# Four residual layers over a 256 x 256 image: the spectra of the kernels' rows stored without a copy, in quarters of the channels, and a third buffer for the sums

## The chip, the core and the metric

The kernel runs on one core of one Trainium2 chip. The metric is the device time of one execution, in microseconds (us). The core has a matrix engine (TensorE, PE in the profile), a vector engine (VectorE, DVE), an activation engine (ScalarE, ACT), a general engine (GpSimd, POOL), a queue engine that issues transfers (SyncE, SP), and 16 DMA engines that move data between HBM and the on-chip memory, SBUF. Each compute engine works through its instructions in the order in which they were built and waits on semaphores. Results of TensorE land in PSUM.

## The reference, cut to what matters

The image x is 1 x 256 x 256 x 128, float32. Four layers follow one another, each of the form x = x + layer(group norm of x).

```python
def _gn(v, G=32, eps=1e-5):
    B_, H_, W_, C_ = v.shape
    g = v.reshape(B_, H_, W_, G, C_ // G)
    m = jnp.mean(g, axis=(1, 2, 4), keepdims=True)
    s = jnp.var(g, axis=(1, 2, 4), keepdims=True)
    return ((g - m) / jnp.sqrt(s + eps)).reshape(v.shape)

x = x + _L0_conv_ref(_gn(x), ...)   # attention along rows, 4 heads of 32, with a pair bias
x = x + _L1_conv_ref(_gn(x), ...)   # 16 steps of a gated recurrence
x = x + _L2_conv_ref(_gn(x), ...)   # triangle product
x = x + _L3_conv_ref(_gn(x), ...)   # 3 x 3 convolution and a dense layer
```

The change touches what layers 0 and 1 need. Layer 0 needs mean and variance of x per group of four channels before anything else. Layer 1 multiplies by the two-dimensional Fourier transforms of two small complex kernels, A and B, of 7 x 7 taps for each of 64 channels, padded to 256 x 256:

```python
def _pad_and_fft(kr, ki, h, w, k):
    kern = kr + 1j * ki
    ph = (h - k) // 2
    pw = (w - k) // 2
    padded = jnp.pad(kern, ((0, 0), (ph, h - k - ph), (pw, w - k - pw)))
    return jnp.fft.fft2(padded, axes=(-2, -1))
A_f = _pad_and_fft(A_real, A_imag, h, w, k)
B_f = _pad_and_fft(B_real, B_imag, h, w, k)
```

## The kernel before

The image is held channel-major in HBM between the stages: 128 channels on the partitions, 65536 pixels along them. The stages run one after another:

- A first pass over x (`statistics`), for sums and sums of squares.
- A second pass (`attention`, its loop over m) that transposes x, normalises it, and stores xT, znT and the pair bias.
- The attention itself (`attend_bounded`), the recurrence, the triangle product and the convolution.

**The first pass.** x comes in 32 chunks of 2048 pixels, 1 MB each, issued by SP (line 243). Most go through a ring of three buffers (`xin`); the last ones in the order of work stay in buffers of their own (`kept`, six of them, line 349), since the second pass begins with them and needn't load them again. Each chunk has two halves of 128 x 1024. For each half VectorE subtracts a shift (written at line 246; the profile shows it as L224, the wrapper that pins it), ScalarE squares the result (line 249; L54 in the profile, the helper), and TensorE adds both up in one PSUM tile, `acc`, with matmuls by ones of 32 columns. The sums of a half take in its differences, `xs`, and the squares, `sq`, of the half before. `xs` and `sq` come from the pool `p0`, which has two buffers of each. These steps are pinned: each engine takes them in the order of the text. In the end VectorE copies `acc` (line 263), and the group statistics follow.

**The spectra of the rows.** The same loop makes the one-dimensional transform of the kernels' seven rows, for A and then for B (`kernel_rows`). After chunks 4, 5, 7, 8, 10, 11, 13 and 14 it calls `spectrum` for A, after 16, 17, 19, 20, 22, 23, 25 and 26 for B. One call treats two channels of each quarter of the 64: TensorE makes `ph` (eight small matmuls, behind the sums of that chunk), and ScalarE copies it to a tile H (line 191), with the 14 rows of quarter k on partitions 32k to 32k+13. H is 128 x 256 x 16, one buffer: 256 points of the transform, 16 channels of a quarter. When a spectrum is complete, GpSimd puts the four quarters of 16 channels beside one another: eight copies (line 197) of 14 x 128 x 16 into the tile HH, four to each half of the 256 points. Two stores (line 198), one to a half, take HH to HBM, to `HD_`, laid out as [2 kernels, 14 rows, 256 points, 64 channels].

**Where the spectra are read.** The recurrence treats four image rows in a block, 64 blocks. `load` fetches for each block, on SP's queue, the image twice (`xf` and the two halves of `xc`) and the spectra for those four rows into `hs`, 128 x 2 x 64 (line 882): four loads, for each kernel n and each r, with two rows of 64 channels for each of 14 partitions. `za` (kernel A) and `zb` (kernel B) are matmuls that use `hs` as weights. The order of the work in a block is a written list of steps with their lags; the loads of a block are issued one block ahead, and `hs` has two buffers, which come free after `zb`.

**Weights.** `attention_weights` is a generator that the loop of the first pass advances: after chunk 1 its loads are out, and at `n == 28` its small computations are recorded. They are not pinned.

Of the kernel before, what the change touches and what calls it, by code (L numbers as in the profile page):

```python
# [9 lines left out]
F32 = mybir.dt.float32  # L10
# [7 lines left out]
P = 128  # L18
N = 256
NPIX = N * N  # L20
NCH = NPIX // 512
NH, HD = 4, 32
KS = 7
HC = P // 2
# [6 lines left out]
class Kernel:  # L31
# [132 lines left out]

    def kernel_rows(self, sp, ps, HD_):


        nc, I = self.nc, self.i
        CG = HC // 4
        tu = self.load(sp, I["c_rows"], "tu")  # L170
        HH = sp.tile([P, N // 2, HC], F32, name="HH")
        H, ka = [], []
        for n, (re, im) in enumerate((("A_real", "A_imag"), ("B_real", "B_imag"))):
            kr, ki = (I["L1_conv_" + y].rearrange("c p q -> p c q") for y in (re, im))
            k = sp.tile([3 * KS, HC, 32], F32, name=f"ka{n}")
            nc.gpsimd.memset(k, 0.0)
            for p0, q0, src in ((0, 0, kr), (0, KS, ki), (KS, 0, ki), (2 * KS, KS, kr)):
                nc.gpsimd.dma_start(k[p0:p0 + KS, :, q0:q0 + KS], src)
            ka.append(k)

        pin = lambda f: lambda *a, **k: self.tc.keep_in_program_order(f(*a, **k))

        def spectrum(g):
            n, g0 = divmod(2 * g, CG)
            if not g0:
                H.append(sp.tile([P, N, CG], F32, name="H"))
            ph = ps.tile([P, 2, N], F32, name="ph", bufs=2)
            for j in range(2):
                for k in range(4):
                    pin(self.mm)(ph[32 * k:32 * k + 32, j], ka[n][:, CG * k + g0 + j, :], tu)  # L190
            pin(nc.scalar.copy)(H[n][:, :, g0:g0 + 2].rearrange("q u c -> q c u"), ph)
            if g0 + 2 == CG:
                for h in range(2):
                    o = slice(64 * n + 32 * h, 64 * n + 32 * h + 2 * KS)
                    u = slice(h * N // 2, (h + 1) * N // 2)
                    for k in range(4):
                        nc.gpsimd.tensor_copy(HH[o, :, CG * k:CG * (k + 1)], H[n][32 * k:32 * k + 2 * KS, u])
                    nc.gpsimd.dma_start(HD_[n][:, u], HH[o])
        return spectrum

    def statistics(self, wp, weights, HD_, kept, src):

        nc, I = self.nc, self.i
        V = nc.vector
        x = I["x"].rearrange("b h w c -> (b h w) c")
        NM, KEPT = NPIX // 2048, len(kept)
        mv = wp.tile([P, 2], F32, name="mvx")
        with ExitStack() as c:  # L210
            sp = c.enter_context(self.pool(name="sp", bufs=1))
            io = c.enter_context(self.pool(name="p0", bufs=2))
            ps = c.enter_context(self.pool(name="p0s", bufs=1, space=PSUM))
            row = sp.tile([1, P], F32, name="row")
            nc.sync.dma_start(row, x[0:1])
            shc = self.column(sp, x[0:1].rearrange("o c -> (o c)"), "shc")
            ones = sp.tile([P, P], F32, name="ones0")
            V.memset(ones, 1.0)
            psh = ps.tile([P, 4, P], F32, name="psh", tag="ph", bufs=2)
            self.mm(psh[:, 0], ones[0:1], row)  # L220
            sh = sp.tile([P, P], F32, name="sh")
            V.tensor_copy(sh, psh[:, 0])
            acc = ps.tile([P, 512], F32, name="acc")
            pin = lambda f: lambda *a, **k: self.tc.keep_in_program_order(f(*a, **k))  # L224
            last, count = None, [0, 0]

            def add_up(*pair):
                for h in range(2):
                    for j, t in enumerate(pair):
                        if t is not None:  # L230
                            o = 64 * j + 32 * h
                            pin(self.mm)(acc[o:o + 32], ones[:, :32], t[:, h * 512:(h + 1) * 512],
                                    start=count[j] < 2, stop=count[j] >= 4 * NM - 2)
                            count[j] += 1

            order = list(range(KEPT, NM)) + list(range(KEPT))
            spectrum, made = None, 0
            for n, m in enumerate(order):
                if m < KEPT:
                    xin = kept[m]  # L240
                else:
                    xin = io.tile([P, 2, 1024], F32, name="xin", bufs=3)
                nc.sync.dma_start(xin, src(m))
                for b in range(2):
                    xs = io.tile([P, 1024], F32, name="xs")
                    pin(V.tensor_tensor)(xs.rearrange("p (t c) -> p t c", t=8), xin[:, b].rearrange("p (t c) -> p t c", t=8),
                                    sh.unsqueeze(1).to_broadcast([P, 8, P]), ALU.subtract)
                    sq = io.tile([P, 1024], F32, name="sqx")
                    pin(self.act)(sq, xs, AF.Square)

                    add_up(xs, last)
                    last = sq
                if n == 1:
                    spectrum = self.kernel_rows(sp, ps, HD_)
                    next(weights)
                elif n == 28:
                    weights = next(weights)
                elif n >= 4 and n % 3 and made < 16:
                    spectrum(made)
                    made += 1  # L260
            add_up(None, last)
            accs = sp.tile([P, 512], F32, name="accs")
            V.tensor_copy(accs, acc)
            sel = sp.tile([P, 2], F32, name="sel")
            V.memset(sel, 0.0)
            V.memset(sel[:64, 0:1], 1.0 / 32 / NPIX)
            V.memset(sel[64:, 1:2], 1.0 / 32 / NPIX)
            pm = ps.tile([P, 2], F32, name="pmx")
            for t in range(4):
                self.mm(pm, accs[:, t * P:(t + 1) * P], sel, start=t == 0, stop=t == 3)  # L270
            V.tensor_copy(mv, pm)
            e = sp.tile([P, 1], F32, name="ex")
            V.tensor_tensor(e, mv[:, 0:1], mv[:, 0:1], ALU.mult)
            V.tensor_tensor(mv[:, 1:2], mv[:, 1:2], e, ALU.subtract)
            V.tensor_tensor(mv[:, 0:1], mv[:, 0:1], shc, ALU.add)
        return mv, weights
# [58 lines left out]

    def attention(self, wp, later, xT, x1T, znT, biasD, HD_, stats1, shift1):
        nc, tc, I = self.nc, self.tc, self.i
# [4 lines left out]
        with ExitStack() as c:  # L342
# [3 lines left out]
            c1 = c.enter_context(ExitStack())  # L346
            kp = c1.enter_context(self.pool(name="kp", bufs=1))

            kept = [kp.tile([P, 2, 1024], F32, name=f"kept{m}") for m in range(6)]
            mv, (w, (lns, lnb), wo, small) = self.statistics(wp, self.attention_weights(wp), HD_, kept, src)  # L350
            with self.pool(name="awq", bufs=2, space=PSUM) as ps0:
                ab, mg, _ = self.group_affine(wp, ps0, None, self.g4, "0", True, mv=mv)
# [14 lines left out]
            io = c1.enter_context(self.pool(name="a1", bufs=3))  # L367
# [70 lines left out]
                    nc.sync.dma_start(biasD[:, s:s + 512], bi[32 * k:32 * k + NH])  # L438

            tc.keep_in_program_order(self.table(LN_EXP))  # L440
            for m in range(6, 8):
                load(m)
            turn(0)
            centre(0, 0)
# [372 lines left out]
    def recurrence(self, x1T, x2T, HD_, stats1, shift1, stats2, shift2):  # L817
# [3 lines left out]
        nc, tc, I = self.nc, self.tc, self.i  # L821
# [3 lines left out]
        with ExitStack() as c:  # L825
# [6 lines left out]
            with self.pool(name="rwp", bufs=2, space=PSUM) as ps0:  # L832
# [9 lines left out]
                for g, add in (("f", 2.0), ("i", 0.0), ("d", 0.0)):  # L842
                    raw, b0 = W["W" + g], W["b" + g]
                    pb = ps0.tile([P, 2], F32, name="rpb" + g, tag="gn")
                    for half in range(2):
                        hs = slice(half * HC, (half + 1) * HC)
# [6 lines left out]
            io = c.enter_context(self.pool(name="r1", bufs=2))  # L853
# [16 lines left out]
            def load(b):  # L870
                d = D[b]
                xf = d["xf"] = io.tile([P, 1024], F32, name="xf", bufs=4)
                nc.sync.dma_start(xf, x1T[:, b * 1024:(b + 1) * 1024])
                xc = d["xc"] = io.tile([P, 2, 512], F32, name="xc")
                for half in range(2):
                    src = x1T[:, b * 1024 + half * 512:b * 1024 + (half + 1) * 512]
                    nc.sync.dma_start(xc[half * HC:(half + 1) * HC], src.rearrange("(r c) n -> c r n", c=HC))
                hs = d["hs"] = io.tile([P, 2, HC], F32, name="hs")
                for n in range(2):
                    for r in range(2):  # L880
                        o = 64 * n + 32 * r
                        nc.sync.dma_start(hs[o:o + 2 * KS], HD_[n, :, b * 4 + r:b * 4 + 4:2, :])

# [581 lines left out]
    def run(self, ctx):  # L1467
        nc, tc = self.nc, self.tc
        const = ctx.enter_context(tc.tile_pool(name="const", bufs=1))
        dram = ctx.enter_context(tc.tile_pool(name="dram", bufs=1, space=DRAM))  # L1470
# [7 lines left out]
        shift2 = const.tile([P, 1], F32, name="shift2")  # L1478
        xT, x1T, x2T, x3T, znT = (image(n) for n in ("xT", "x1T", "x2T", "x3T", "znT"))
        biasD = dram.tile([NH, NPIX], F32, name="biasD")  # L1480
        HD_ = dram.tile([2, 2 * KS, N, HC], F32, name="HD")
        prodD = image("prodD")
        self.early = {n: [const.tile([P, 2], F32, name=f"early{k}{n}") for k in range(2)] for n in "3"}
        later = ctx.enter_context(self.pool(name="lw", bufs=1))
# [71 lines left out]
```

## Time and profile before

| what | us |
|---|---|
| median of 3 runs (5156.23 to 5160.0) | 5156.7 |
| the profiled execution, its own time | 5160.9 |
| its span on the core | 5159.1 |
| first pass, to the copy of `acc` | 0 to 166 |
| second pass | 172 to 490 |
| attention | 500 to 1740 |
| recurrence | 1740 to 3260 |
| triangle product and convolution | 3260 to 5159 |
| GpSimd's 16 copies at line 197 | 39.6 in all |
| mean granted TensorE clock, share of full speed | 0.984 |

In the first 172 us the 64 subtractions at line 224 keep VectorE busy for 95.1 us, the 64 squares ScalarE for 65.8, the 16 copies of `ph` for 16.4. The profile shows spans of instructions on each engine; a matmul's end is modelled, so a busy TensorE isn't always at its peak. The idle time before an instruction is given with what ended it, and of several semaphores only the one that came last is named. Stages differ: what a change is worth is read where the changed lines run, not from a mean over the span.

### The profile page before, as it was taken

Reading aid. Unit: us, or ns where it says so; the run is one execution under the profiler, and the core shown is the slowest. Engines: PE = TensorE matmul, PEld = TensorE weight load, DVE = VectorE, ACT = ScalarE, POOL = GpSimd, SP = SyncE. Lnnn points to the kernel's source line nnn. Section 1 sums busy time; section 2 is a strip of 40 time slices with the busy share of each in tenths; the row PEclk is TensorE's granted clock in tenths of the full one; section 3 lists DMA queues with packets and bytes.
Section 4 is the critical chain, followed back from the end, with each engine's and each line's share of the span. In section 5 each row is a group of like instructions: output and inputs, shape, how many; then the busy total and the mean of one; then the engine's idle time right before and its main releaser. Section 6 shows DMA issues by size and latency. Waiting matters only on the chain.

```text
span 5159.1 us, 78300 instructions
## 1 busy us (share of the span) xinstructions
PE 4960.6 (96%) x31357; PEld 2701.3 (52%) x31357; DVE 4119.8 (80%) x4797; ACT 3497.7 (68%) x4948; POOL 451.8 (9%) x612
## 2 busy tenths in 40 slices
PE   7999999999999899999999999899999989989999
PEld 1344555555555333333333333229999953339999
DVE  5666999999999699999999999775333527779886
ACT  4444888888888799999999999453333357762110
POOL 2332000000000000000000000240111010000000
PEclk8899999999999899999999999999999999999999
DMA  8696222222222122222222221688667668865432
GB/s 276 207 337 251 75 87 83 79 87 84 84 80 87 63 68 71 67 71 67 71 67 72 69 72 55 234 316 282 230 228 247 237 259 333 322 230 194 140 120 66
DMA packets 180108, 782.45 MB, mean 152 GB/s; under 512 B 31713, under 2 KB 35119, under 8 KB 130535
## 3 DMA queue, kind: packets, MB, share of 16 engines
q1 hardware_dynamic: 122254, 506.60, 29.4%
q0 software_dynamic: 56192, 270.42, 14.2%
q8 instruction: 250, 4.10, 0.3%
q14 instruction: 116, 0.94, 0.1%
q10 hardware_dynamic: 1296, 0.40, 0.0%
HBM read 505.99 MB, written 271.32 MB: 151 GB/s over the span
## 4 chain that ended last, share of the span: by engine, by line
PE 55%; DVE 28%; issue 5%; ACT 1%; DMA 1%; POOL 0%; SPq 0%; POOLq 0%; DVEq 0%; ACTq 0%
PE z L60 9%; PE m L60 7%; PE nd L60 7%; PE sc L60 5%; PE zc L60 4%; PE po L60 4%; DVE tr L898 3%; DVE t L895 3%; DVE y L895 3%; DVE p L895 3%; DVE yf L895 3%; PE ppq L60 3%; PE ppv L60 2%; PE px L60 2%; PE pe L60 2%
## 5 line engine op out<-in xcount | busy, mean ns | idle before, releaser
L563 DVE TENSOR_TENSOR e<-sc,bT 128x1024 f32<-128x1024 f32 x512 | 603.0, 1219 | 52.5 <-PE sc L60 51.3
L54 ACT ACTIVATE e<-e 128x1024 f32<-128x1024 f32 x512 | 540.4, 1055 | 63.3 <-DVE e L563 54.0
L1058 DVE TENSOR_TENSOR LR<-z,sg 128x512 f32<-128x512 f32 x256 | 268.0, 1048 | 365.2 <-ACT sg L54 358.9
L60 PE MATMUL m<-U,v 128*128 128x128 f32 x4608 | 516.6, 276 | 6.6 <-DVE v L1405 6.6
L60 PEld LDWEIGHTS m<-U,v 128*128 128x128 f32 x4608 | 516.4, 192 | 6.7 <-DVE v L1405 6.7
L60 PE MATMUL z<-wf,zt 128*128 128x128 f32 x4096 | 460.0, 276 | 2.6 <-DVE zn L1058 1.4
L60 PEld LDWEIGHTS z<-wf,zt 128*128 128x128 f32 x4096 | 459.6, 193 | 3.7 <-DVE zn L1058 2.2
L54 ACT ACTIVATE sg<-z 128x512 f32<-128x512 f32 x256 | 152.8, 597 | 309.4 <-PE z L60 307.0
L54 ACT ACTIVATE sq<-zs 128x1024 f32<-128x1024 f32 x192 | 202.4, 1054 | 196.6 <-DVE zs L374 156.8
L60 PE MATMUL sc<-tq,tk 32*128 32x256 f32 x4096 | 298.1, 403 | 2.9 <-DVE e L563 2.0
L563 DVE TENSOR_TENSOR ks<-e 128x1024 f32<-128x1024 f32 x256 | 300.8, 1216 | 0.0
L60 PE MATMUL nd<-e,tv 128*32 128x256 f32 x4096 | 272.1, 383 | 0.0
L60 PEld LDWEIGHTS sc<-tq,tk 32*128 32x128 f32 x4096 | 187.2, 185 | 160.6 <-issue 97.1
L54 ACT ACTIVATE dn<-dn 128x512 f32<-128x512 f32 x384 | 241.9, 630 | 13.3 <-DVE dn L563 2.6
L60 PE MATMUL av<-y,ident 128*128 128x512 f32 x384 | 191.4, 607 | 44.8 <-DVE y L895 44.8
L60 PE MATMUL po<-LR 128*128 128x256 f32 x1024 | 222.2, 380 | 6.9 <-DVE LR L1058 6.9
L1442 ACT COPY m4s<-m 128x512 f32<-128x512 f32 x32 | 18.7, 584 | 286.5 <-PE m L60 286.5
L60 PEld LDWEIGHTS po<-LR 128*128 128x128 f32 x1024 | 194.1, 190 | 34.2 <-DVE LR L1058 7.7
L60 PE MATMUL bx<-p,ident 128*128 128x512 f32 x384 | 193.3, 612 | 0.0
L54 ACT ACTIVATE o<-po 128x256 f32<-128x256 f32 x256 | 84.3, 381 | 145.3 <-issue 108.4
L60 PEld LDWEIGHTS nd<-e,tv 128*32 128x32 f32 x4096 | 120.3, 110 | 109.8 <-issue 44.3
L866 ACT ACT_TABLE_LOAD x132 | 169.4, 1283 | 1.6
(369 smaller groups left out, 10354.4 us busy)
## 6 DMA issues: line engine op xcount, KB each, us to landing
zt<-znT SPq DMA_DIRECT2D x128, 1024.0 KB
znT<-zn POOLq DMA_DIRECT2D x64, 1024.0 KB, 5.4
xin<-x2T SPq DMA_DIRECT2D x64, 1024.0 KB
xin<-in_x_dram SPq DMA_DIRECT2D x52, 1024.0 KB
xr<-x3T SPq DMA_DIRECT2D x46, 768.0 KB
xT<-xo POOLq DMA_DIRECT2D x32, 1024.0 KB, 9.5
xr<-xT SPq DMA_DIRECT2D x64, 512.0 KB
zn<-znT SPq DMA_DIRECT2D x64, 512.0 KB
```

The source lines that it names most:

```text
L54: return self.nc.scalar.activation(out, in_, func, bias=bias, scale=scale, **kw)
L60: return self.nc.tensor.matmul(out, lhsT, rhs, start=start, stop=stop)
L563: pin = lambda f: lambda *a, **k: tc.keep_in_program_order(f(*a, **k))
L866: pin(nc.scalar.preload_act_table_set(want))
L895: pin(V.tensor_tensor(out, a, b_, op))
L898: pin(V.scalar_tensor_tensor(out, a, k, b_, op0, op1))
L1058: pin = lambda f: lambda *a, **k: tc.keep_in_program_order(f(*a, **k))
L1442: nc.scalar.copy(m4, m[4])
```

## The change

- HH and GpSimd's copies go. Each quarter of H is stored as it stands: four stores for a spectrum, of 14 partitions x 256 points x 16 channels, in place of two. H has two buffers.
- `HD_` is laid out as [2 kernels, 14 rows, 4 quarters, 256 points, 16 channels].
- The recurrence fetches, for each kernel, each r and each of two rows j, the four quarters of 16 channels: eight loads to a block instead of four, each with runs of 16 channels (64 bytes) where there were runs of 64 (256 bytes).
- The pool `p0` has three buffers each of `xs` and `sq`, not two.
- Seven chunks are kept between the first two passes, not six; the loads of the second pass start one later.
- The small computations with the attention's weights are recorded after chunk 9, not 28.

```diff
@@ kernel_rows
         CG = HC // 4
         tu = self.load(sp, I["c_rows"], "tu")
-        HH = sp.tile([P, N // 2, HC], F32, name="HH")
...
             if not g0:
-                H.append(sp.tile([P, N, CG], F32, name="H"))
+                H.append(sp.tile([P, N, CG], F32, name="H", bufs=2))
...
             if g0 + 2 == CG:
-                for h in range(2):
-                    o = slice(64 * n + 32 * h, 64 * n + 32 * h + 2 * KS)
-                    u = slice(h * N // 2, (h + 1) * N // 2)
-                    for k in range(4):
-                        nc.gpsimd.tensor_copy(HH[o, :, CG * k:CG * (k + 1)], H[n][32 * k:32 * k + 2 * KS, u])
-                    nc.gpsimd.dma_start(HD_[n][:, u], HH[o])
+                for k in range(4):
+                    nc.gpsimd.dma_start(HD_[n, :, k], H[n][32 * k:32 * k + 2 * KS])
@@ statistics
-            io = c.enter_context(self.pool(name="p0", bufs=2))
+            io = c.enter_context(self.pool(name="p0", bufs=3))
...
-                elif n == 28:
+                elif n == 9:
                     weights = next(weights)
@@ attention
-            kept = [kp.tile([P, 2, 1024], F32, name=f"kept{m}") for m in range(6)]
+            kept = [kp.tile([P, 2, 1024], F32, name=f"kept{m}") for m in range(7)]
...
-            for m in range(6, 8):
+            for m in range(7, 9):
                 load(m)
@@ recurrence, load
                         o = 64 * n + 32 * r
-                        nc.sync.dma_start(hs[o:o + 2 * KS], HD_[n, :, b * 4 + r:b * 4 + 4:2, :])
+                        for j in range(2):
+                            nc.sync.dma_start(hs[o:o + 2 * KS, j].rearrange("q (k c) -> q k c", k=4),
+                                              HD_[n, :, :, b * 4 + r + 2 * j, :])
@@ run
-        HD_ = dram.tile([2, 2 * KS, N, HC], F32, name="HD")
+        HD_ = dram.tile([2, 2 * KS, 4, N, HC // 4], F32, name="HD")
```

## The prediction

> **What bounds the kernel now.** I read first the table of busy times in 40 slices, to find where the kernel is not at the pace of one engine; then the timeline of VectorE, ScalarE and GpSimd over the first 185 us, since the edited lines run there; then busy times by stretch for the later stages that read what the change writes. Columns of a timeline line: start, busy time, engine, line, operation with its tiles, count, and in brackets the idle time before it and what ended that.
>
> The first pass over x takes 166 us. VectorE's subtractions show why (a "x2" line is one chunk of 2048 pixels):
>
> ```profile
> 70.56 2.42 DVE L224 TENSOR_TENSOR xs<-xin,sh 128x1024 f32<-128x1024 f32 x2 [1.62 <-ACT sqx L54]
> 74.61 10.63 DVE L224 TENSOR_TENSOR xs<-xin,sh 128x1024 f32<-128x1024 f32 x4 [1.63 <-ACT sqx L54]
> 95.20 1.23 DVE L224 TENSOR_TENSOR xs<-xin,sh 128x1024 f32<-128x1024 f32 x1 [9.96 <-ACT sqx L54]
> ...
> 115.44 2.36 DVE L224 TENSOR_TENSOR xs<-xin,sh 128x1024 f32<-128x1024 f32 x2 [8.36 <-DMA xin<-in_x_dram]
> ...
> 140.42 21.94 DVE L224 TENSOR_TENSOR xs<-kept,sh 128x1024 f32<-128x1024 f32 x8 [1.63 <-ACT sqx L54]
> 166.10 0.69 DVE L263 COPY accs<-acc 128x512 f32<-128x512 f32 x1 [3.73 <-PE acc L60]
> ```
>
> One subtraction takes 1.21 us, but 2.7 in the line at 74.61 and in the line at 140.42. GpSimd's timeline gives the partner, ScalarE's the second wait:
>
> ```profile
> 73.79 13.20 POOL L197 COPY HH<-H 14x2048 f32<-14x2048 f32 x5 [62.99 <-ACT H L181]
> ...
> 87.53 5.74 POOL L197 COPY HH<-H 14x2048 f32<-14x2048 f32 x3
> ...
> 139.60 13.20 POOL L197 COPY HH<-H 14x2048 f32<-14x2048 f32 x5 [45.50 <-ACT H L181]
> ...
> 153.30 7.99 POOL L197 COPY HH<-H 14x2048 f32<-14x2048 f32 x3
> ```
>
> ```profile
> 62.15 1.02 ACT L181 COPY H<-ph 128x512 f32<-128x512 f32 x1 [1.23 <-PE ph L60]
> 62.97 1.99 ACT L54 ACTIVATE sqx<-xs 128x1024 f32<-128x1024 f32 x2
> 65.38 2.25 ACT L54 ACTIVATE sqx<-xs 128x1024 f32<-128x1024 f32 x2 [0.41 <-DVE xs L224]
> 68.66 1.02 ACT L181 COPY H<-ph 128x512 f32<-128x512 f32 x1 [1.03 <-PE ph L60]
> ...
> 93.31 1.01 ACT L181 COPY H<-ph 128x512 f32<-128x512 f32 x1 [12.57 <-POOL HH L197]
> ```
>
> Both slow stretches lie inside GpSimd's two sets of eight copies. The first copy of the second spectrum (93.31) waits 12.57 us for the single H, and squares and subtractions stand behind it in order. What follows up to 118 is aftermath: TensorE restarts at a clock of 0.50 (93 to 104), and the chunk at 115.44 is late because its load queued behind six kept chunks issued meanwhile.
>
> The second pass gives TensorE's pace: the stores of xT stand 9.54 us apart to the hundredth, whether DMA is 66% busy (200 to 220) or 96%:
>
> ```profile
> 230.10 0.54 POOL L396 DMA_DIRECT2D xT<-xo  x1 [1.87 <-ACT xo L374]
> ...
> 239.64 0.54 POOL L396 DMA_DIRECT2D xT<-xo  x1 [1.87 <-ACT xo L374]
> ```
>
> In the recurrence VectorE is busy without a gap, and a block's four hs loads are issued well ahead (busy times by stretch, then SP's and TensorE's timelines):
>
> ```profile
> 1800.00:2400.00 600.00, 584.00 (x1960) 194.49 (x1957) 600.00 (x748) 578.30 (x850) 13.82 (x26) 1.00 0.22 70
> ```
>
> ```profile
> 2426.42 1.60 SPq L882 DMA_DIRECT2D hs<-HD  x4
> ```
>
> ```profile
> 2439.56 1.13 PE L60 MATMUL za<-ev,hs 14*128 14x512 f32 x4
> ```
>
> **What the Trainium skill says.** "SBUF — State Buffer", section "Who interferes with whom": a VectorE instruction with two SBUF inputs contends with a GpSimd instruction that reads SBUF; the later one is blocked until the other ends. Line 224 has two SBUF inputs, line 197 reads SBUF, and the trace agrees: 2.7 to 2.9 us against 1.21, one copy's length apart. "DMA: Bandwidth & Descriptors", "Specifications": full rate needs 512 B a run or more. The hs runs were 256 B and become 64; the trace shows the former hidden and says nothing of the latter. "TensorE: Matmul & The Clock Gate", "What's actually happening": a mostly idle TensorE falls to half clock. The trace agrees: 0.50 after the stall, the matmuls of acc 1.06 us instead of 0.62.
>
> **The change, part by part.** Chunks are numbered 0 to 31 in order of work; spectrum steps follow 4, 5, 7, 8 and so on to 14 (first spectrum) and 16 to 26 (second).
>
> *Copies gone, H twice.* Sixteen copies, 39.6 us of GpSimd, go; GpSimd keeps issuing stores, eight of 224 KB instead of four of 448, at 0.52 us each: 4 us instead of 2, in which VectorE may lose a few tenths; the same bytes. No copy on ScalarE waits for H any more. So the pace seen from 36 to 73 us goes on to the end.
>
> *Third xs and sq buffer.* The pace is three chunks in 10.56 us (copy at 62.15 to copy at 72.71). Most of it is a loop through ScalarE and TensorE: square, its sums, the next ph, copy, next square (4.05 us each for two chunks). That loop doesn't depend on these buffers. Only the 0.41 us before the squares at 65.38 (their input wasn't ready, since xs was still in use) goes: 10.14 us.
>
> *Sum to the end of the pass.* The copy after chunk 14 starts at 72.71; three threes have passed since chunk 5: 72.71 - 3 x 0.42 = 71.4. Four threes more: 71.4 + 4 x 10.14 = 112.0 for the copy after chunk 26; its 0.82 ends at 112.8. Chunks 27 to 31 have no step. With three buffers three of their ten subtractions are done by then; the square frees the next at 113.8, seven follow at 1.21: 122.4 with semaphores; last square 1.06, 123.4. From there to line 263 it took 2.58 us with the sums at half clock; at full clock about 1.5: 124.9 against 166.10. Gain 41.2 us.
>
> *DMA as cover.* The pace needs a chunk (1.049 MB) each 3.38 us. Rates at a DMA share of 0.84 to 1.00 were 299 to 398 GB/s; at 322 (20 to 36 us, share 0.99) a chunk takes 3.26, at 354 (340 at share 0.96) 2.96. Just enough. The order on SP changes: all 25 streamed chunks go before the seven kept ones, which wait for no buffer. The last streamed one is issued when chunk 21 is used up, about 91.5; eight chunks then land by 91.5 + 2.2 + 8 x 2.96 to 3.26 = 117 to 120; the second spectrum's 0.92 MB (2.6 to 2.9) falls among them. Wanted for the last pair: 120.0. So 0 to 3 us late; I take 1.2.
>
> *weights at 9 instead of 28; kept 7.* None of it is pinned: in the built order VectorE has these small instructions at the same place, around the third chunk, in both. Nothing. The second pass loads one chunk less, but TensorE sets it: nothing; were its cover gone, 3 us of gain.
>
> *Recurrence.* Per block eight hs loads instead of four, 448 runs of 64 B instead of 112 of 256. SP issues them in 3.2 us instead of 1.6, behind them only xf, which has four buffers. za wants its four loads 13.1 us after the first issue: hidden behind VectorE. Once, at the start, block 0 is not covered: there the four took 2.45 us to issue, za stood from 1746.1 behind zd until 1749.7, and its third and fourth load leave no later than before; but more runs are in flight. 0 to 3 us; I take 1.0, since zd ends at 1749.74 anyway.
>
> Sum: -41.2 + 1.2 + 1.0 = -39.0 us, on a profiled execution of 5160.9 us (span 5159.1), which lies 4.2 above the median of the runs, 5156.7. Median: 5117.7, say 5118.
>
> **Rivals.** *HBM sets the pass.* If the rate stays at 322 GB/s throughout: the fourth load leaves at about 20.6, 29 chunks x 3.26 and 1.84 MB of spectra (5.7) end at 120.8, landing 2.2, last pair and sums 5: 128. Gain 38, less 1 in the recurrence; with stores that delay loads at a bad moment, up to 10 less. 5120 to 5129. For it: little slack. Against it: the shares below 0.9.
>
> *The slow subtractions are not GpSimd's doing* but go with the low clock. Then only the wait for H goes, 12.57 us and about 2 behind it: 5142. Against it: at 95.20, clock 0.50, a subtraction takes 1.23.
>
> *Slower: the gather is late in each block.* Place: za in the recurrence. It decides where the first four hs loads take over 13.1 us to land; at 13.7 the 64 blocks have eaten 39 us, at 14.3 it is 77: 5195. For it: four times the runs. Against it: before, four loads landed within 6.8 us beside full-size loads; a doubling is covered.
>
> *It doesn't do what it says*: GpSimd's built order has eight stores and no copy; only a hidden wait could keep the old times. Under 1 in 100.
>
> **Numbers.** Forecast 0.80 (5110 to 5124); HBM 0.12; low clock 0.03; gather 0.04; no change 0.01. Low end: the gain of 41.2 with nothing lost and a few us at restarts that no longer run at half clock, 5108; high end: HBM's, 5129. A measurement of this kernel tells about 0.2% (10 us) from no change: faster 0.95, same 0.01, slower 0.04.
>
> **What would show it.** Right: line 263's copy at 122 to 131; no subtraction above 1.3 us after 36; copies to H 4.05 and 6.1 apart up to chunk 26; TensorE's clock near 1.00 from 20 to 120; stores of xT 9.54 apart; recurrence VectorE busy without a gap, block time 23.3. Wrong: subtractions waiting for xin from chunk 16 on (HBM), subtractions of 2.7 us without GpSimd copies (clock), za waiting for hs (gather).

## The result, and the profile after

| | before | after |
|---|---|---|
| median of 5 runs each, side by side, us | 5156.7 | 5126.9 |
| ratio of after to before, 95% interval | | 0.9941 [0.9926, 0.9955] |
| profiled execution, us (its span) | 5160.9 (5159.1) | 5127.0 (5125.2) |
| first subtraction of the first pass, us | 18.19 | 23.20 |
| copy of `acc`, us | 166.10 | 133.64 |
| between these two, us | 147.9 | 110.4 |
| from the copy of `acc` to the end of the span, us | 4993.0 | 4991.6 |

The kernel is 30 us faster, 0.6%. The forecast was 5118 with a range of 5108 to 5129: the time lies inside the range, near its slow end. It lies outside the band that the forecast gave its own mechanism (5110 to 5124), and inside what the rival "HBM sets the pass" would give (5120 to 5129). Line numbers after the change are four lower from about line 190 on (L224 is L220, L263 is L259), three lower in the recurrence (L882 is L879).

VectorE's timeline of after (start, busy time, line, operation, tiles, count, idle time before and what ended it):

```profile
68.00 3.54 DVE L220 TENSOR_TENSOR xs<-xin,sh 128x1024 f32<-128x1024 f32 x3 [1.65 <-ACT sqx L54]
...
91.54 2.36 DVE L220 TENSOR_TENSOR xs<-xin,sh 128x1024 f32<-128x1024 f32 x2 [6.13 <-DMA xin<-in_x_dram]
...
123.26 8.08 DVE L220 TENSOR_TENSOR xs<-kept,sh 128x1024 f32<-128x1024 f32 x7 [1.65 <-ACT sqx L54]
133.64 0.69 DVE L259 COPY accs<-acc 128x512 f32<-128x512 f32 x1 [2.30 <-PE acc L60]
```

A subtraction takes 1.2 us throughout: the last seven take 8.08 us where eight took 21.94 before. One long wait is left, and it stands at a new place: at 91.54 chunk 19 is 6.13 us late. Shorter waits for loads, up to 1.62 us, lie between 43 and 77 us. GpSimd and ScalarE of after:

```profile
77.41 2.06 POOL L194 DMA_DIRECT2D HD<-H  x4 [66.45 <-ACT H L181]
122.66 1.97 POOL L194 DMA_DIRECT2D HD<-H  x4 [43.19 <-ACT H L181]
```

```profile
66.10 1.02 ACT L181 COPY H<-ph 128x512 f32<-128x512 f32 x1 [1.24 <-PE ph L60]
66.92 3.88 ACT L54 ACTIVATE sqx<-xs 128x1024 f32<-128x1024 f32 x4
...
76.08 1.04 ACT L181 COPY H<-ph 128x512 f32<-128x512 f32 x1 [1.24 <-PE ph L60]
76.92 3.89 ACT L54 ACTIVATE sqx<-xs 128x1024 f32<-128x1024 f32 x4
82.04 1.02 ACT L181 COPY H<-ph 128x512 f32<-128x512 f32 x1 [1.23 <-PE ph L60]
```

The first copy of the second spectrum (82.04) waits 1.23 us for TensorE, as every other does, and for no H; before, it waited 12.57. Three chunks take 9.98 us (66.10 to 76.08). GpSimd's copies are gone, its stores are left. Busy times by stretch show what the DMA engines did around the first four stores (the columns are PE, PEld, DVE, ACT and POOL, then TensorE's clock, DMA share and GB/s):

```profile
76.00:80.00 4.00, 3.82 (x32) 0.85 (x32) 3.22 (x3) 3.92 (x5) 2.06 (x4) 1.00 1.19 398
80.00:83.00 3.00, 3.00 (x35) 0.85 (x32) 1.55 (x2) 1.77 (x3) 0.00 (x0) 1.00 0.90 169
83.00:86.00 3.00, 2.84 (x28) 0.60 (x30) 2.36 (x2) 1.85 (x3) 0.00 (x0) 1.00 0.90 225
...
92.00:95.00 3.00, 2.17 (x12) 0.55 (x16) 2.80 (x3) 2.06 (x2) 0.00 (x0) 0.56 0.66 261
```

From 80 to 86 the engines are 90% busy but move only 169 and 225 GB/s. Chunk 19, wanted at 85.4 (91.54 - 6.13), lands only after that. After the wait TensorE restarts at a clock of 0.56. The packets of the queues show whose time this was (packets, MB, share of the 16 engines; q1 carries SP's loads, q0 GpSimd's stores; first from 80 to 83, then from 60 to 100 us):

```profile
q0 software_dynamic: 56, 0.34, 76.2%
q1 hardware_dynamic: 44, 0.16, 13.6%
```

```profile
q1 hardware_dynamic: 2881, 11.14, 77.0%
q0 software_dynamic: 128, 0.92, 14.0%
```

The four stores moved 0.92 MB and took 14.0% of 40 us, as much as all 16 engines for 5.6 us. At what the loads took for a MB (77.0% of 40 us for 11.14 MB, 2.76 us) it would have been 2.5 us.

The two later places. The second pass keeps its pace of 9.55 us (POOL's timeline); in the recurrence VectorE is busy without a gap (by stretch), eight hs loads are issued in 6.71 us, and `za` doesn't wait (SP's and TensorE's timelines):

```profile
226.16 0.54 POOL L392 DMA_DIRECT2D xT<-xo  x1 [1.87 <-ACT xo L370]
235.71 0.54 POOL L392 DMA_DIRECT2D xT<-xo  x1 [1.87 <-ACT xo L370]
```

```profile
1760.00:2400.00 640.00, 623.38 (x2095) 207.26 (x2095) 640.00 (x797) 616.94 (x909) 14.49 (x28) 1.00 0.22 68
```

```profile
2417.17 6.71 SPq L879 DMA_DIRECT2D hs<-HD  x8
```

```profile
2430.31 1.13 PE L60 MATMUL za<-ev,hs 14*128 14x512 f32 x4
```

From the first `za` to the last `zb` it is 1489.56 us in both profiles (1749.67 to 3239.23; 1717.11 to 3206.67).

So the profiled execution is 33.9 us shorter: 37.5 are gained between the first subtraction and the copy of `acc`, 1.4 after it, and 5.0 are lost before the first subtraction. The medians differ by less, 29.8 us here and 34.1 when the pair was timed once more (after_again below). Two things need an explanation: where the forecast gain of 41.2 in the pass lost 3.7, and what the late start is.

### The profile page after: what moved, and what is told of

It reads as the page before. It is cut to its first block, busy times and chain, and to the rows that moved or that the text cites. A ratio compares the mean times of both kernels' runs of the same rounds, so it can differ in the third digit from the quotient of the medians.

```text
span 5125.2 us, 78589 instructions
## 1 busy us (share of the span) xinstructions
PE 4948.5 (97%) x31357; PEld 2702.7 (53%) x31357; DVE 4100.7 (80%) x4797; ACT 3496.2 (68%) x4948; POOL 414.2 (8%) x600
## 4 chain that ended last, share of the span: by engine, by line
PE 56%; DVE 28%; issue 5%; ACT 1%; DMA 1%; POOL 0%; POOLq 0%; DVEq 0%; SPq 0%; ACTq 0%
PE z L60 9%; PE m L60 7%; PE nd L60 7%; PE sc L60 5%; PE po L60 4%; PE zc L60 4%; DVE tr L896 3%; DVE t L893 3%; DVE y L893 3%; DVE p L893 3%; DVE yf L893 3%; PE ppq L60 3%; PE ppv L60 2%; PE px L60 2%; PE pe L60 2%
```

## The experiments

The theory: the gain comes from GpSimd's copies leaving VectorE alone, from the second H and from the third buffer, in this order; what is missing is the wait for chunk 19, which the first spectrum's stores cause. Rivals: the loads of x can't keep the pace anyway (HBM sets the pass); the gather in the recurrence costs something; the start is an effect of the change.

All times are medians in us, each beside the kernel before on the same chip. "Pass" is from the first subtraction to the copy of `acc`, in the profiled execution; "rest" from there to the end of its span.

| run | median (n) | before | ratio [95%] | first subtraction | pass | rest |
|---|---|---|---|---|---|---|
| before_again | 5159.9 (1) | 5158.1 | | 23.08 | 148.5 | 4986.5 |
| after_again | 5126.0 (5) | 5160.1 | 0.9933 [0.9920, 0.9947] | 23.42 | 111.4 | 4988.9 |
| two_sums | 5131.1 (5) | 5160.1 | 0.9944 [0.9931, 0.9958] | 23.79 | 118.1 | 4987.0 |
| one_H | 5136.1 (4) | 5158.1 | 0.9953 [0.9936, 0.9969] | 17.91 | 125.5 | 4987.4 |
| dummy_copies | 5144.2 (6) | 5158.1 | 0.9968 [0.9956, 0.9981] | 23.64 | 132.4 | 4987.4 |
| late_store | 5124.3 (5) | 5160.1 | 0.9930 [0.9917, 0.9944] | 24.02 | 112.2 | 4989.7 |
| delayed_store | 5117.5 (5) | 5160.5 | 0.9917 [0.9904, 0.9931] | 23.20 | 105.8 | 4987.8 |
| pinned_weights | 5136.9 (5) | 5160.1 | 0.9954 [0.9940, 0.9967] | 10.96 | 132.8 | 4989.9 |
| no_taps | 5112.9 (4) | 5160.5 | 0.9910 [0.9895, 0.9925] | 13.49 | 110.4 | 4985.7 |
| late_taps | 5118.8 (5) | 5164.9 | 0.9912 [0.9898, 0.9925] | 18.74 | 107.5 | 4990.8 |
| gather_twice | 5122.4 (4) | 5158.1 | 0.9922 [0.9905, 0.9938] | 23.37 | 112.3 | 4990.0 |
| gather_four | 5500.6 (1) | 5160.5 | | 17.58 | 112.3 | 5369.0 |

**How far one execution can be trusted.** Nothing is edited in these two runs.

> The kernel before, profiled once more, for its start: if the 18.19 us of its first subtraction is one draw of a varying start, it is now anywhere from 17 to 24 us; if it belongs to that kernel, it is 18 again. The rest of its first pass is expected the same: two slow stretches, 148 us from first subtraction to line 263.

> The changed kernel once more, timed beside the one before. The gain was forecast at 39.0 us; the first comparison gives 29.8 between the medians and 33.9 between the two profiled spans. In its profile the first subtraction starts at 23.20 us, in that of before at 18.19, and both wait there for the same small load, m. If that start varies from execution to execution, it lies between 18 and 24 again and on no fixed side, and the ratio of the times lands near 0.993. If the change itself makes the start later, it is at 23 or more again and the ratio stays at 0.994.

The pass repeats to about 1 us before (147.9 and 148.5) and 2 us after (110.4 and 111.4; 112.2 to 112.3 in late_store, gather_twice and gather_four, whose edits do nothing to it). The start does not: of two executions of before, one has its first subtraction at 18.2 and one at 23.1; of the variants of after that leave the start alone, two show 17.6 and 17.9, the others 23.2 to 24.0. So the 5.0 us lost at the start of the profiled execution are not shown to be the change's. The rest differs by 6.5 us between two executions of before. In what follows the pass is the sharper measure, the median the fairer one.

**GpSimd's copies alone.** The sixteen copies come back, into a tile that nothing reads; H keeps two buffers, the layout and the stores stay. One chunk fewer is kept, to make room.

```diff
+                for h in range(2):
+                    for k in range(4):
+                        nc.gpsimd.tensor_copy(HH[32 * h:32 * h + 2 * KS], H[n][32 * k:32 * k + 2 * KS, h * N // 2:(h + 1) * N // 2])
                 for k in range(4):
                     nc.gpsimd.dma_start(HD_[n, :, k], H[n][32 * k:32 * k + 2 * KS])
```

> The changed kernel with GpSimd's sixteen copies put back, into a tile that nobody reads; the stores still take H, H still has two buffers, and six chunks are kept for room. It does work that leads to nothing. By the prediction the copies block VectorE: the subtractions beside them take 2.7 to 2.9 us instead of 1.2, two stretches of about 21 us with eight subtractions each where the pace would give twelve: 7 to 12 us each, 15 to 24 us slower than the changed kernel. If the slow subtractions went with TensorE's low clock, they stay at 1.2 and the time is that of the changed kernel within 3 us.

The pass takes 132.4 us against 110.4 and 111.4; the median is 17 to 18 us higher. GpSimd's and VectorE's timelines:

```profile
78.97 22.78 POOL L196 COPY HH<-H 14x2048 f32<-14x2048 f32 x8 [68.04 <-ACT H L182]
...
132.34 21.69 POOL L196 COPY HH<-H 14x2048 f32<-14x2048 f32 x8 [28.58 <-ACT H L182]
```

```profile
78.97 26.12 DVE L224 TENSOR_TENSOR xs<-xin,sh 128x1024 f32<-128x1024 f32 x11 [2.00 <-ACT H L182]
...
133.09 19.18 DVE L224 TENSOR_TENSOR xs<-kept,sh 128x1024 f32<-128x1024 f32 x7 [1.65 <-ACT sqx L54]
```

The tile isn't read, no copy to H waits for these copies, and only GpSimd's own stores stand behind them. Yet the subtractions in these lines take 2.37 and 2.74 us each on average (26.12 / 11; 19.18 / 7), where after has 1.2. This is the contention that the Trainium skill describes ("SBUF — State Buffer", section "Who interferes with whom"), now seen with only the copies put back and one kept chunk fewer, and it costs 21 to 22 us of the pass.

**H and the third buffer alone.** Two edits, one in each run:

```diff
-                H.append(sp.tile([P, N, CG], F32, name="H", bufs=2))
+                H.append(sp.tile([P, N, CG], F32, name="H"))
```

> The changed kernel with one H instead of two. The copy after chunk 16 then waits until the four stores of the first spectrum have read H. They were issued over 2 us and landed in 4 to 11 us: the copy waits some 6 to 10 us more, and loads are late for part of that time anyway: 3 to 9 us slower. If the second H is hidden by that wait for loads, under 2 us.

```diff
-            io = c.enter_context(self.pool(name="p0", bufs=3))
+            io = c.enter_context(self.pool(name="p0", bufs=2))
```

> The changed kernel with two buffers of xs and sq instead of three. By the prediction the third takes 0.42 us from each of seven threes of chunks and some of the end: 3 to 5 us slower than the changed kernel, threes of 10.5 us instead of 10.0. Rival: with HBM as the bound the threes are no longer set by these buffers, and the time is the same within 1 us.

With one H the pass is 14 to 15 us longer and the median 9 to 10, more than the 3 to 9 expected. ScalarE waits for the stores to be through, and VectorE later for a load (ScalarE's, then VectorE's timeline of one_H):

```profile
85.76 1.01 ACT L181 COPY H<-ph 128x512 f32<-128x512 f32 x1 [8.58 <-DMA HD<-H]
```

```profile
109.45 2.36 DVE L220 TENSOR_TENSOR xs<-xin,sh 128x1024 f32<-128x1024 f32 x2 [11.05 <-DMA xin<-in_x_dram]
```

With two sums the pass is 6.7 us longer than after_again's, the median 5.2. Three chunks take 10.55 us again (copies to H at 57.62, 68.18 and 78.73), because the squares' input is late every third chunk, as it was before (ScalarE's timeline of two_sums):

```profile
60.85 2.25 ACT L54 ACTIVATE sqx<-xs 128x1024 f32<-128x1024 f32 x2 [0.41 <-DVE xs L220]
...
71.41 2.25 ACT L54 ACTIVATE sqx<-xs 128x1024 f32<-128x1024 f32 x2 [0.41 <-DVE xs L220]
```

So the third buffer gives 0.55 us per three chunks, 3.9 us over seven threes. Another 1.7 us lie behind the last copy to H: from there to the copy of `acc` it is 14.0 us (127.84 to 141.87) instead of 12.3 (121.35 to 133.64). Copies, H and sums taken back one at a time cost 21, 14 and 7 us; that is 42 against 37.5 for all. The prices aren't independent, since each run has its own waits for late loads (3.71 us at 116.57 in dummy_copies, 11.05 in one_H, 5.93 at 95.49 in two_sums).

**The wait for chunk 19.** The first attempt to move the first spectrum's stores only recorded them later:

```diff
-                for k in range(4):
-                    nc.gpsimd.dma_start(HD_[n, :, k], H[n][32 * k:32 * k + 2 * KS])
+                for m in range(2 if n else 0):
+                    for k in range(4):
+                        nc.gpsimd.dma_start(HD_[m, :, k], H[m][32 * k:32 * k + 2 * KS])
```

> The changed kernel with the first spectrum's four stores held back and issued with the second's, after chunk 26. Theory: the 6.1 us for which a subtraction waits for xin at 91.5 come from the first four stores at 77.4, which take DMA time from the loads. Then that wait is gone, chunk 26's copy of H stands about 5 us nearer to chunk 5's, and the time is 3 to 6 us shorter, less what eight stores at the end cost. Rival: the rate of HBM alone is too low for the pace; then the wait stays, somewhere between chunks 16 and 24, and the time is the same.

GpSimd has nothing else to do, so it issued the four stores as soon as H[0] was full, at 79.32, and the wait stayed (GpSimd's, then VectorE's timeline of late_store):

```profile
79.32 2.06 POOL L195 DMA_DIRECT2D HD<-H  x4 [68.38 <-ACT H L181]
```

```profile
93.13 2.36 DVE L221 TENSOR_TENSOR xs<-xin,sh 128x1024 f32<-128x1024 f32 x2 [6.03 <-DMA xin<-in_x_dram]
```

The edit was inert, and the run counts as one more of the changed kernel. The second attempt makes the stores really wait: ScalarE, after its last copy to H[1], writes one element of H[0] onto itself, and the stores of H[0] depend on that.

```diff
+                    if m == 0:
+                        pin(nc.scalar.copy)(H[0][:, 0:1, 0:1], H[0][:, 0:1, 0:1])
                     for k in range(4):
```

> The changed kernel with the first spectrum's stores really held back: after chunk 26 ScalarE writes one element of the first H onto itself, and the stores wait for that. (In late_store they had left as soon as the first spectrum was complete, 7 us ahead of the wait for xin as before, so that kernel tested nothing.) If the stores at 77 cause the wait of 6 us at 91.5, it is gone, the pass is 4 to 6 us shorter from its first subtraction to its end (105 to 107 instead of 110.4 and 111.4), and the median 3 to 6 us lower, unless 1.84 MB of stores at the end cost it again. If loads alone are too slow, there is still a wait for xin, and the pass takes 110 to 112.

All eight stores leave together, after the last load of x is issued (GpSimd's, then VectorE's timeline of delayed_store):

```profile
117.90 4.02 POOL L197 DMA_DIRECT2D HD<-H  x8 [107.02 <-ACT H L181]
```

```profile
84.42 2.40 DVE L223 TENSOR_TENSOR xs<-xin,sh 128x1024 f32<-128x1024 f32 x2 [1.28 <-ACT sqx L54]
88.47 4.67 DVE L223 TENSOR_TENSOR xs<-xin,sh 128x1024 f32<-128x1024 f32 x4 [1.65 <-ACT sqx L54]
...
128.97 0.69 DVE L262 COPY accs<-acc 128x512 f32<-128x512 f32 x1 [2.30 <-PE acc L60]
```

From 60 us to the copy of `acc` no subtraction waits for a load, though the same 32 chunks are loaded; the first subtraction is at 23.20 as in after, so the copy of `acc` at 128.97 instead of 133.64 is 4.7 us gained in the pass (5.6 against after_again). Busy times by stretch for the time in which after's stores began:

```profile
76.00:80.00 4.00, 3.84 (x37) 0.83 (x26) 2.35 (x3) 3.45 (x4) 0.00 (x0) 1.00 0.90 316
```

The same share of 0.90 that carried 169 GB/s beside the stores carries 316 without them. This decides between the rivals: the loads keep the pace by themselves, and the first spectrum's stores caused the wait. The median, 5117.5, is the lowest of a kernel that computes everything; its ratio, 0.9917 against 0.9941 and 0.9933 of the two measurements of after, has an interval that overlaps theirs. The 4.7 us are shown by the profile, the full 8 or 9 between the medians are not.

**The start.** First, VectorE's small computations with the weights are pinned behind chunk 9, where the text has them; in before and after they run around the first three chunks. The wrapper V pins what is called through it; all of these calls go through it.

```diff
+        V = Pinned(tc, nc.vector)
...
-            nc.vector.tensor_scalar_mul(w[nm], raws[nm], f)
+            V.tensor_scalar_mul(w[nm], raws[nm], f)
```

> The changed kernel with VectorE's small instructions for the attention's weights pinned where the text now records them, after chunk 9, instead of ahead of the first chunk, where they wait for m. If the first chunks are held by m alone, the first subtraction starts at 12 to 16 instead of 18 to 23, and the pass ends up to 8 us earlier, less a chain of some 27 small instructions with round trips to TensorE and ScalarE, about 6 to 10 us, of which the prefetched chunks hide none for VectorE: between 5 us faster and 4 us slower. If x itself arrives no earlier than m, since the small loads of the kernels' taps fill the DMA engines, the first subtraction stays at 17 to 22 and the chain is added: 4 to 10 us slower.

Nothing is ahead of the first subtraction now, so it runs at 10.96, but the second chunk isn't there (VectorE's timeline):

```profile
10.96 2.36 DVE L229 TENSOR_TENSOR xs<-xin,sh 128x1024 f32<-128x1024 f32 x2 [4.76 <-DMA xin<-in_x_dram]
23.30 2.36 DVE L229 TENSOR_TENSOR xs<-xin,sh 128x1024 f32<-128x1024 f32 x2 [9.98 <-DMA xin<-in_x_dram]
```

The start hangs on loads, and the computations, moved into the busy pass, cost it 9 to 10 us at the copy of `acc` (143.7 against 134.8 and 133.6). What holds the loads? In no_taps the eight loads of the 7 x 7 taps are left out, so both spectra come out as zero:

```diff
-            for p0, q0, src in ((0, 0, kr), (0, KS, ki), (KS, 0, ki), (2 * KS, KS, kr)):
-                nc.gpsimd.dma_start(k[p0:p0 + KS, :, q0:q0 + KS], src)
```

> The changed kernel without the eight loads of the kernels' taps, 3584 runs of 28 bytes: it leaves the taps at zero, so the spectra are zero, and is there for the time of the start alone. If these loads fill the DMA engines from 8 to 23 us (share 1.0 at 90 GB/s), m and x arrive early without them: the first subtraction at 8 to 13 instead of 18 to 24, and the whole 6 to 12 us shorter. If the start is set by the order of the other loads, the first subtraction stays at 18 or 23.

The first subtraction moves from 23.2 to 13.5, which is outside what the start does by itself (17.6 to 24.0), and the time falls to 5112.9. The stretch from 12 to 16 us, in after and then in no_taps:

```profile
12.00:16.00 4.00, 0.00 (x0) 0.00 (x0) 0.09 (x1) 0.00 (x0) 0.00 (x0) 1.00 0.96 107
```

```profile
12.00:16.00 4.00, 2.23 (x9) 0.95 (x8) 3.81 (x10) 1.18 (x2) 0.00 (x0) 1.00 0.60 239
```

The tap loads have runs of seven values, 28 bytes. With them the engines are 96% busy at 107 GB/s, but little of that is the taps' own time. By queue, in the same stretch, after and then no_taps (q0 carries the taps, q1 SP's loads):

```profile
q1 hardware_dynamic: 90, 0.37, 84.7%
q0 software_dynamic: 79, 0.04, 7.5%
```

```profile
q1 hardware_dynamic: 250, 0.95, 59.9%
```

A packet of SP's loads took 0.60 us beside the taps (84.7% of 16 x 4 us, by 90) and 0.15 without them (59.9%, by 250). So the taps slow the other loads' packets; why they do isn't shown. The last run is delayed_store with kernel B's four tap loads held until ScalarE has passed chunk 8:

```diff
+            if g == 3:
+                pin(nc.scalar.copy)(ka[1][:, 0:1, 0:2 * KS], ka[1][:, 0:1, 0:2 * KS])
+                for p0, q0, src in taps:
+                    nc.gpsimd.dma_start(ka[1][p0:p0 + KS, :, q0:q0 + KS], src)
```

> The first spectrum's stores are late as in the run before it, and of the eight tap loads the four of kernel B (read from chunk 16 on) now wait for ScalarE to pass chunk 8, some 50 us into the pass. If the tap loads hold the start by filling the DMA engines (28-byte runs), half of them give half of what leaving all out gave (first subtraction 13.5 instead of 23.2): the first subtraction at 17 to 19, and 4 to 6 us off the end if the pass can absorb the other four while it runs: 5112 to 5114. The rival: the pass has no such slack, because the four loads cost the DMA engines about 6 us at whatever moment they run; then a subtraction waits 4 to 6 us for xin after chunk 8 and the time stays at 5116 to 5120. A third: the start is held by something else, the first subtraction stays at 23.

The first subtraction comes at 18.74, about half way, as the theory has it; but starts of 17.6 to 18.2 occur without the edit too, so one execution doesn't show that the edit did it. The loads issued from 53.84 to 57.01 then delay x (GpSimd's, then VectorE's timeline):

```profile
53.84 0.80 POOL L196 DMA_DIRECT2D ka<-in_L_conv_B_real_dram  x1 [46.16 <-ACT ka L182]
```

```profile
65.14 2.36 DVE L228 TENSOR_TENSOR xs<-xin,sh 128x1024 f32<-128x1024 f32 x2 [3.46 <-DMA xin<-in_x_dram]
...
126.20 0.69 DVE L267 COPY accs<-acc 128x512 f32<-128x512 f32 x1 [2.30 <-PE acc L60]
```

Of 4.5 us at the start 2.8 are left at the copy of `acc` (126.20 against 128.97). The ratio to the kernel before, 0.9912 against 0.9917, can't tell a gain from none. So it isn't shown that the four loads are cheaper at the later place. They still cost something there, as the wait of 3.46 us shows.

**The gather.** The loads of `hs` are cut further: sixteen to a block with runs of 32 bytes, then 32 with runs of 16.

```diff
-                            nc.sync.dma_start(hs[o:o + 2 * KS, j].rearrange("q (k c) -> q k c", k=4),
-                                              HD_[n, :, :, b * 4 + r + 2 * j, :])
+                            for s in (slice(0, 8), slice(8, 16)):
+                                nc.sync.dma_start(hs[o:o + 2 * KS, j].rearrange("q (k c) -> q k c", k=4)[:, :, s],
+                                                  HD_[n, :, :, b * 4 + r + 2 * j, s])
```

> The changed kernel with each load of hs cut in two again, sixteen loads to a block with runs of 32 bytes. The eight loads were measured at 0.784 us of issue each (four took 0.38 each before), 6.7 us to a block. Theory: SP's issue is the price and hides as long as a block's loads fit: sixteen take 12.5 us, the first eight, which za needs, 6.3, within the 13.1 us that za leaves: same time within 2 us, except 2 to 5 at the first block, where za now comes after the eighth load. Rival: landing grows with the runs; then za waits in each block, 64 times 1 us or more: over 60 us slower.

> The changed kernel with each load of hs cut in four: 32 loads to a block with runs of 16 bytes. At 0.784 us each SP issues for 25.1 us, with xf and xc about 26.9, more than the 23.3 us of a block: SP becomes the bound of the recurrence, a block takes 26.5 to 28 us, 64 times 3.2 to 4.7: 200 to 300 us slower than the changed kernel. If issue is not the price, under 20 us.

Sixteen loads cost nothing: 5122.4, and 1489.6 us from the first `za` to the last `zb`, as before; the 2 to 5 us expected at the first block don't appear. SP's timeline of gather_twice, then of gather_four:

```profile
2416.56 13.72 SPq L880 DMA_DIRECT2D hs<-HD  x16
```

```profile
2400.04 26.95 SPq L880 DMA_DIRECT2D hs<-HD  x32
2427.11 0.46 SPq L869 DMA_DIRECT2D xf<-x1T  x1
2427.67 1.35 SPq L873 DMA_DIRECT2D xc<-x1T  x2
2429.11 27.37 SPq L880 DMA_DIRECT2D hs<-HD  x32
```

At 32 loads SP issues without a pause, 29.07 us to a block (2400.04 to 2429.11), where a block took 23.3. 64 blocks times 5.8 us are about 370 us, against a measured loss of 374 or 375 to 5126.9 or 5126.0 (one execution). That is more than the 200 to 300 expected, since an issue took 0.84 us and not 0.784. Now `za` does wait (TensorE's timeline), and VectorE has gaps (by stretch, 510 us busy of 640):

```profile
2444.47 2.04 PE L60 MATMUL za<-ev,hs 14*128 14x512 f32 x2 [4.51 <-DMA hs<-HD]
```

```profile
1760.00:2400.00 640.00, 565.32 (x1639) 195.04 (x1638) 510.27 (x632) 485.93 (x716) 11.16 (x21) 0.89 0.21 55
```

So the rival "the gather is late in each block" is possible, but not at the eight loads of the change, and at 32 its price is the issue on SP, which leaves no pause. With about 0.84 us an issue and 2 us for xf and xc, an estimate of where it begins is (23.3 - 2) / 0.84 = 25 loads; the change has eight.

## Why the prediction was right, and where it was off

The time is inside the range, but the range reached that far only because its slow end was taken from the rival. The forecast's own band ended at 5124, and both measurements of after miss it (5126.9 and 5126.0). Of its signs, the copy of `acc` was to come at 122 to 131 and came at 133.64, and the sign against it, a subtraction that waits for `xin` from chunk 16 on, was there. The cause of that wait was another one than the sign stood for. So most of the mechanism was right, one term was too small, and that the total stayed in the range is in part luck.

- *Copies gone, H twice*: right, and by its own mechanism. The copies cost 21 us and the single H 14 when put back alone. Rival "the slow subtractions are not GpSimd's doing" falls with dummy_copies: copies that no other engine waits for are enough.
- *Third xs and sq buffer*: right in kind, 0.55 us per three chunks instead of 0.42. Over seven threes that is 0.8 to 0.9 us more gain.
- *Sum to the end of the pass*: 124.9 - 18.19 = 106.7 us after the first subtraction, before DMA is counted. delayed_store, in which no load is late after 60 us, took 105.8. The 0.9 between are 0.8 from the line above and 0.5 behind the copy after chunk 26 (12.4 instead of 12.9), less 0.4 lost before the copy after chunk 5 (23.3 instead of 22.8).
- *DMA as cover*: this is the term that was mis-sized. I took 1.2 us of lateness (0 to 3), and looked for it in the last eight chunks with the second spectrum's stores among them. The last eight were on time. It happened at chunk 19, behind the first spectrum's stores, as 6.13 us, and cost 4.7. The fault was to leave the first spectrum's stores out, to charge stores by their bytes at the common rate (0.92 MB, 2.6 to 2.9 us; their packets took 5.6 us of all engines), and to read a share near 0.9 as a rate near 300 GB/s: beside these stores it was 169. The rival "HBM sets the pass" named it in its last clause ("stores that delay loads at a bad moment") and gave a time that fits; its main clause, a rate of 322 GB/s that can't keep up, is refuted by delayed_store.
- *Recurrence*: 1.0 us taken, 0.0 measured at the start and in the blocks. The issue time was underestimated, 0.84 us a load instead of 0.40, and hidden all the same: 6.7 us of 13.1.
- *weights at 9, kept 7*: nothing is seen of them. The small computations run around the first three chunks in both, though not in quite the same order among the subtractions, and neither has a run of its own. pinned_weights shows that real movement of that work would have lost 9 to 11 us.
- *Second pass*: 9.55 us a chunk, unchanged.
- *Clock*: near 1.00 as expected, except 0.56 after the wait at 91.5 and 0.86 from 30 to 36 us.
- The start was in no step of the sum. The forecast took the profiled execution with its first subtraction at 18.2 as typical; the profile of after has it at 23.2.

The sum from profile to profile: -39.0 forecast, + 3.5 (DMA), - 0.9 (pass without late loads), - 1.0 (recurrence), + 5.0 (start), - 1.4 (rest) = -33.8; measured -33.9. Start and rest differ as much between two executions of one kernel. That the sum closes to 0.1 us is therefore chance.

## What to carry to other kernels

An engine's copy that no other engine waits for can still be the most expensive thing on the page, if it reads the memory that another engine's two-input operation reads; here removing it was worth more than the buffers. When a pass has just enough DMA for its pace, don't charge a store by its bytes: look at when it leaves and what engine time its packets take, and try to let it leave after the last load. The gather with short runs was paid here in the issuing queue's time per load, so compare loads x issue with the length of the block that hides them.

## What the runs showed of the hardware that was not expected

- An hs load took SP 0.84 us to issue (6.71 / 8) with 56 runs of 64 bytes, 0.40 (1.60 / 4) with 28 runs of 256 bytes; with 32 and 16 bytes a run it stayed at 0.86 and 0.84 (13.72 / 16, 26.95 / 32). The bytes don't set it; whether the number of runs does isn't shown, since the shape of the access changed too.
- Stores of 14 partitions with 16 KB each brought the engines to 169 GB/s at a share of 0.90, where loads of 128 partitions alone gave 316 at the same share. A MB of these stores took 6.1 us of all 16 engines (5.6 / 0.92), a MB of loads 2.76. A possible reason, argued and not tested: by the Trainium skill ("SBUF — State Buffer", section "Door 1: The DMA port swizzle") the DMA rate depends on how many of 16 ports the partitions reach, and by its table partitions 0 to 13, 32 to 45, 64 to 77 and 96 to 109 reach eight.
- Beside loads with runs of 28 bytes the engines stood at a share of 0.96 and 107 GB/s from 12 to 16 us. These loads' own packets took only 7.5% of the engines' time; the packets of the other loads took four times as long as without them (0.60 us and 0.15). What makes the start fall at 18 in some executions and at 23 in others stays open.
